# Second four tiles projected in the front of an attention and expert kernel, and a group's sums copied out of their bank in one instruction

## The chip, the cores and the metric

The kernel runs on one core of a Trainium2 chip. Its engines are named as in the profile: PE (TensorE, matmuls; PEld is its loading of weights), DVE (VectorE), ACT (ScalarE), POOL (GpSimd) and SP (SyncE, which here issues transfers). The metric is the device time of one execution in microseconds, as the median of several executions. Beside it there is one profiled execution, whose trace gives every instruction's start and duration.

## The reference

Two residual layers over `x` of 2 x 1024 tokens and 256 features, everything in fp32:

```python
x = x + attn(layernorm(x))      # 16 query heads, 4 key/value heads of 16 features
x = x + ffn(layernorm(x))       # shared expert + 60 experts, top 4

# attn
q = rms_norm(x @ q_kernel); k = rms_norm(x @ k_kernel); v = x @ v_kernel
q, k = rope(q), rope(k)                                   # per head of 16
probs = softmax(einsum('btkgh,bskh->bkgts', q / 4, k))    # no mask
out = einsum('bkgts,bskh->btkgh', probs, v).reshape(B, T, 256) @ out_kernel

# ffn
shared = (silu(x @ g.T) * (x @ u.T)) @ d.T * sigmoid(x @ shared_gate.T)
weights, sel = top_k(softmax(x @ gate.T), 4)
out = shared + sum over the 60 experts of cw_e * ((silu(x @ w1_e.T) * (x @ w3_e.T)) @ w2_e.T)
```

## The kernel before, in words

Tokens are cut into 16 tiles of 128, of which the first eight are batch 0. Tiles are projected in sets of four (`RB`). Set 0 is projected in the front by `project_first`; sets 1 to 3 are projected by the generator `project`, a piece at a time, between the steps of attention.

**The front.** PE multiplies the identity by itself five times (`warm`, line 253), subtracts the weights' means (`center`), and projects set 0: queries to two score buffers (`pq`, `project_to`, line 274), keys and values to a third (`pk`). ACT squares the queries for their norms, copies keys and values out (`kv`, line 409) and squares the keys. DVE takes the variances of x, turns queries and keys (rope), and runs a Newton iteration for the inverse roots (`norm`). PE meanwhile runs 11 more matmuls on the identity, transposes the padded keys (`ktp`, line 345), runs 7 more on the identity, and transposes the scaled queries (`qtp`, line 358). ACT and DVE copy the transposes to `kT` and `qT`, and DVE writes the values, times their norm, to `vaug` (line 335).

**The steps of attention.** There are 128, in the order batch, half of the queries (`qb`), `jp`, `jj`, and key tile `s` (eight). A step has four score matmuls, each on its own 32 rows of the array and 512 queries wide (line 545), into two of three score buffers of two banks each; two exponentials on ACT, 128x1024 each (line 560); and four averages with `vaug`, each on its own 32 columns of the array, summed over the eight steps of a group in the one bank of `ps_av` (line 1068). PE's order is: scores of step r+1, then one piece of other work (`fill`; not in a group's last step, nor in step 1), then the averages of step r. The pieces come from a list: set 1 from step 0 on, then sets 2 and 3, later the output projection and the routing of tokens.

For set 1 the pieces were: keys and values projected to the `misc` bank (`pk`), copied by DVE (line 451), turned and squared, variances (step 0); key transposes (steps 2 and 3), the norm and `vaug` with the first of them; queries of two tiles projected (`pq`), copied by DVE to `u` (line 492) and squared, with half of their turning on POOL (steps 4 and 5); the queries' norm; scaling and query transposes. The `misc` bank is one for all.

**The end of a group.** After a group's eighth step the sums hold numerators and denominators of four heads in turn. With `jj` 0, DVE copies them to `num` (line 578) and later shuffles `num` to `den`. With `jj` 1, DVE copies the odd rows over `num` under a mask (line 585) and shuffles the sums into `den2` (line 586), both out of the bank; the rest (a masked copy, four reciprocals, two products to `encT`) stands in the list `slow`, from which one piece is taken after each of the next seven steps. The output projection reads `encT` nine and ten steps after a group's end with `jp` 1 and `jj` 1. After the last step the list is emptied at once, and PE goes on with the shared expert, where two more output projections are put between.

PE, ACT, DVE and POOL keep the order in which the code names their instructions. SP issues the inputs in front, tiles 4 to 7 of the transposed x (line 144) after the small tables, and then the clearing of the experts' buffers. Behind attention come half of the shared expert, the ranks of the experts, the 60 experts, and the other half of the shared expert.

Of the kernel before, what the change touches and what calls it, by code (L numbers as in the profile page):

```python
# [16 lines left out]
P = 128  # L17
# [6 lines left out]
QB = 512  # L24
# [27 lines left out]
def attention_moe_kernel(  # L52
# [196 lines left out]
    def warm(n):  # L249

        to = bank(P, "warm")
        for _ in range(n):
            nc.tensor.matmul(to, lhsT=ident, rhs=ident, start=True, stop=True)
# [55 lines left out]
        return rope_sb[:, tiles[0] % TPB : tiles[0] % TPB + len(tiles), :]  # L309

    def key_tiles(n):
        kv = pj.tile([P, RB, 2, NKV, H], F32, tag="kv", bufs=1, name=f"kv{n}")
        k1 = pj.tile([P, RB, NKV, H], F32, tag="k1", bufs=1, name=f"k1_{n}")
        k2 = pj.tile([P, RB, NKV, H], F32, tag="k2", bufs=1, name=f"k2_{n}")
        return kv, k1, k2

    def turn_keys(tiles, uk, k1, k2):

        pos = rope_of(tiles)
        nc.vector.tensor_tensor(  # L320
            k1, uk, pos[:, :, None, 0:H].to_broadcast([P, RB, NKV, H]), ALU.mult
        )
        for to, fr, s0 in TURNS:
            nc.vector.tensor_tensor(
                k2[:, :, :, to : to + HH],
                uk[:, :, :, fr : fr + HH],
                pos[:, :, None, s0 : s0 + HH].to_broadcast([P, RB, NKV, HH]),
                ALU.mult,
            )
        pad = kpad[tiles[0] // RB % 2][:, :, H:].rearrange("p t (g w) -> p t g w", g=NKV)  # L330
        nc.vector.tensor_add(pad[:, :, :, 0:H], k1, k2)
# [9 lines left out]
    def keys(tiles, jj, bank, copy):  # L341

        tp = bank(RB * P, f"ktp{tiles[0]}_{jj}").rearrange("p (t n) -> p t n", t=RB)
        for k in range(RB):
            nc.tensor.transpose(
                tp[:, k, :], kpad[tiles[0] // RB % 2][:, k, H - H * jj :][:, 0:P], ident
            )
        c0 = tiles[0] % TPB * P
        copy(
            kT[tiles[0] // TPB][:, jj, c0 : c0 + RB * P], tp.rearrange("p t n -> p (t n)")  # L350
        )
# [15 lines left out]
    def project_first():  # L367


        tiles = range(RB)  # L370
        pos = rope_of(tiles)
        two = [P, 2, NH, H]
        pq = {}
        for k in range(0, RB, 2):
            pq[k] = any_bank(2 * NH * H, f"pq{k}").rearrange("p (t n) -> p t n", t=2)
            for t in range(2):
                project_to(pq[k][:, t], k + t, 0, NH * H)
        variance(tiles)
        t2 = pj.tile([P, RB, NH * H], F32, tag="t2", bufs=1, name="t2_0")
        for k in range(0, RB, 2):  # L380
            for t in range(2):
                sq = pj.tile([P, NH * H], F32, tag="sq", bufs=1, name=f"sq{k + t}")
                nc.scalar.activation(
                    sq,
                    pq[k][:, t],
                    AF.Square,
                    scale=(NH * H) ** -0.5,
                    accum_out=ss[:, 0, k + t : k + t + 1],
                )
            of_k = pos[:, k : k + 2]  # L390
            q1 = pj.tile([P, 2, NH * H], F32, tag="q1", name=f"q1_{k}")
            nc.vector.tensor_tensor(
                heads(q1), heads(pq[k]), of_k[:, :, None, 0:H].to_broadcast(two), ALU.mult
            )
            for to, fr, s0 in TURNS:
                nc.vector.tensor_tensor(
                    heads(t2[:, k : k + 2])[:, :, :, to : to + HH],
                    heads(pq[k])[:, :, :, fr : fr + HH],
                    of_k[:, :, None, s0 : s0 + HH].to_broadcast([P, 2, NH, HH]),
                    ALU.mult,  # L400
                )
            (nc.vector if k else nc.gpsimd).tensor_tensor(
                t2[:, k : k + 2], q1, t2[:, k : k + 2], ALU.add
            )
        pk = any_bank(RB * 2 * NKV * H, "pk0").rearrange("p (t n) -> p t n", t=RB)
        for k in tiles:
            project_to(pk[:, k], k, NH * H, 2 * NKV * H)
        kv, k1, k2 = key_tiles(0)
        nc.scalar.copy(kv.rearrange("p t w g h -> p t (w g h)"), pk)
        for k in tiles:  # L410

            sq = pj.tile([P, NKV * H], F32, tag="sqk1", bufs=1, name=f"sqk{k}")
            nc.scalar.activation(
                sq,
                kv[:, k, 0].rearrange("p g h -> p (g h)"),
                AF.Square,
                scale=NKV**-0.5,
                accum_out=ss[:, 1, k : k + 1],
            )
        warm(11)  # L420
        turn_keys(tiles, kv[:, :, 0], k1, k2)
        keys(tiles, 0, any_bank, nc.scalar.copy)
        keys(tiles, 1, any_bank, nc.scalar.copy)
        warm(7)
        norm(tiles, 0, 3)
        for k in tiles:
            r = rqk[:, 0, k : k + 1]
            if k < 2:
                nc.vector.tensor_scalar_mul(t2[:, k], t2[:, k], r)
            else:  # L430
                nc.scalar.activation(t2[:, k], t2[:, k], AF.Copy, scale=r)
        for k in tiles:
            queries(k, 1, t2[:, k : k + 1], any_bank, (nc.vector.tensor_copy, nc.scalar.copy)[k % 2])
        values(tiles, kv)

    def project(tiles):

        copy = nc.vector.tensor_copy
        set_ = tiles[0] // RB
# [2 lines left out]
        if b == 1:  # L442
            for k in range(0, RB, 2):
                variance(tiles[k : k + 2])
                yield

        pk = bank(RB * 2 * NKV * H, f"pk{set_}").rearrange("p (t n) -> p t n", t=RB)
        for k, i in enumerate(tiles):
            project_to(pk[:, k], i, NH * H, 2 * NKV * H)
        kv, k1, k2 = key_tiles(set_)  # L450
        copy(kv.rearrange("p t w g h -> p t (w g h)"), pk)
        uk = kv[:, :, 0]
        of_k = uk.rearrange("p t g h -> p t (g h)")

# [26 lines left out]
                values(tiles, kv)  # L481
            yield

        u = pj.tile([P, RB, NH * H], F32, tag="u", bufs=1, name=f"u{set_}")

        t2 = pj.tile([P, RB, NH * H], F32, tag="t2", bufs=1, name=f"t2_{set_}")
        pos = rope_of(tiles)
        for k in range(0, RB, 2):
            pq = bank(2 * NH * H, f"pq{tiles[k]}").rearrange("p (t n) -> p t n", t=2)
            for t in range(2):  # L490
                project_to(pq[:, t], tiles[k + t], 0, NH * H)
            copy(u[:, k : k + 2], pq)  # L492
            for t in (k, k + 1):
                sq = pj.tile([P, NH * H], F32, tag="sq", bufs=1, name=f"sq{tiles[t]}")
                nc.vector.scalar_tensor_tensor(
                    sq,
                    u[:, t],
                    1.0 / (NH * H),
                    u[:, t],
                    ALU.mult,  # L500
                    ALU.mult,
                    accum_out=ss[:, 0, tiles[t] : tiles[t] + 1],
                )
            for to, fr, s0 in TURNS:
                for t in (k, k + 1):
                    nc.gpsimd.tensor_tensor(  # L506
                        heads(t2[:, t : t + 1])[:, 0, :, to : to + HH],
                        heads(u[:, t : t + 1])[:, 0, :, fr : fr + HH],
                        pos[:, t, None, s0 : s0 + HH].to_broadcast([P, NH, HH]),
                        ALU.mult,  # L510
                    )
            yield
# [59 lines left out]
    def group_end(av, encT, jp, jj):  # L572

        nonlocal num, den
        if jj == 0:
            num = ends_of.tile([P, QB], F32, tag="num", bufs=2, name="num")
            den = ends_of.tile([P, QB], F32, tag="den", bufs=2, name="den")
            nc.vector.tensor_copy(num, av)
            slow.append(lambda d=den, n=num: nc.vector.stream_shuffle(d, n, SWAP))
            return  # L580
        while slow:
            slow.pop(0)()
        n, d = num, den
        den2 = ends_of.tile([P, QB], F32, tag="den2", bufs=1, name="den2")
        nc.vector.copy_predicated(n, odd_sb.to_broadcast([P, QB]), av)
        nc.vector.stream_shuffle(den2, av, SWAP)  # L586
        slow.append(lambda: nc.vector.copy_predicated(d, odd_sb.to_broadcast([P, QB]), den2))
        for c in range(0, QB, P):
            slow.append(lambda c=c: nc.vector.reciprocal(d[:, c : c + P], d[:, c : c + P]))
            if c // P % 2:  # L590
                h = slice(c - P, c + P)
                slow.append(lambda h=h: nc.vector.tensor_mul(encT[:, jp, h], n[:, h], d[:, h]))
# [403 lines left out]
    with tc.manual_schedule(engines={mybir.EngineType.PE}), ExitStack() as both:  # L996
# [6 lines left out]
        warm(5)  # L1003
        center(0, NH * H)
        center(NH * H, 3 * P)
        project_first()
        late = project(range(RB, TPB))

# [382 lines left out]
```

## Time and profile before

| | us |
|---|---|
| median of three runs | 678.12 (677.0 to 678.4) |
| the profiled execution itself | 678.74 |
| its span on the core | 676.9 |
| front, up to the first score matmul | 19.8 |
| PE busy in 0 to 19.8, of 19.8 | 16.60 |
| PE busy in 19.8 to 46 (26.2 long) | 25.83 |
| PE busy in 155 to 290 (135 long), ACT in the same | 133.54, 112.05 |
| PE busy in 400 to 640 (240 long) | 236.84 |
| the end of the chain that ended last | shared expert on PE, from 614.5 to 673.3 |

In the lines of the timeline the columns are start, length, engine, line, operation, output and inputs, shape, and the number of instructions merged; in brackets is the engine's idle time before it and who ended it. A long score or projection matmul in fp32 has two records. The waits give who waited for whom, the total, how often and the longest. Rows of one line give count, shortest/median/longest duration in ns, and the first and last start in us.

### The profile page before, as it was taken

The page shows a single profiled execution, that of the slowest core. Times are in us where ns is not written, and L with a number is a line of the kernel's source. Part 1 is how long each engine was busy: PE and PEld are TensorE (multiplying, and loading weights), DVE is VectorE, ACT ScalarE, POOL GpSimd, SP SyncE. Part 2 cuts the span into 40 slices and gives each one's busy share as a digit, 9 for nine tenths or more (in the row PEclk, how much of TensorE's full clock was granted, in tenths as well). Part 3 has the DMA queues.
Part 4 walks back from the last instruction along what each step waited for, and adds up shares of the span by engine and source line. Part 5 has one row for each costly group of instructions (what it writes and reads, how often), then busy time and mean ns, then how long its engine had stood idle before and what let it go on. Part 6 is the DMA issues. An engine that isn't in the chain of part 4 may idle for free. (4 is left out here: it accounts for less than half of the span.)

```text
span 676.9 us, 12425 instructions
## 1 busy us (share of the span) xinstructions
PE 663.9 (98%) x4156; PEld 375.9 (56%) x4157; DVE 361.7 (53%) x1404; ACT 355.7 (53%) x503; POOL 185.7 (27%) x250
## 2 busy tenths in 40 slices
PE   8999999999999999999999998999999999999997
PEld 7432332442224223233235477898998989885466
DVE  5653755427154376556657755444444434543984
ACT  3678778768986787877862400333333333332210
POOL 4020020011000034533135451444444454543000
PEclk9999999999999999999999999999999999999999
DMA  8999930002100011211011084799989899933951
GB/s 274 294 285 298 333 124 1 1 1 92 42 1 1 0 43 42 75 51 50 9 51 66 34 317 163 252 292 296 298 284 307 286 287 293 299 90 113 309 178 48
DMA packets 64275, 106.33 MB, mean 157 GB/s; under 512 B 7417, under 2 KB 51209, under 8 KB 64210
## 3 DMA queue, kind: packets, MB, share of 16 engines
q1 hardware_dynamic: 55010, 86.57, 39.6%
q0 software_dynamic: 7680, 17.32, 7.4%
q10 hardware_dynamic: 1520, 1.64, 0.7%
q8 instruction: 33, 0.54, 0.3%
q14 instruction: 32, 0.26, 0.1%
HBM read 64.13 MB, written 42.45 MB: 157 GB/s over the span
## 5 line engine op out<-in xcount | busy, mean ns | idle before, releaser
L545 PE MATMUL sc<-qT,kT 32*128 32x512 f32 x1024 | 160.3, 639 | 0.8 <-DVE vaug L335 0.5
L560 ACT ACTIVATE ex<-sc,rqk 128x1024 f32<-128x1024 f32 x128 | 134.2, 1111 | 36.8 <-PE sc L545 35.1
L1068 PE MATMUL av<-ex,vaug 128*32 128x512 f32 x1024 | 137.3, 604 | 2.6 <-DVE den L586 1.8
L560 ACT ACTIVATE ex<-sc 128x1024 f32<-128x1024 f32 x128 | 124.1, 1022 | 28.2 <-PE sc L545 24.6
L933 POOL DMA_INDIRECT yt<-ys,dst x96 | 92.8, 966 | 115.2 <-ACT ys L1207 67.5
L545 PEld LDWEIGHTS sc<-qT,kT 32*128 32x128 f32 x1024 | 52.7, 183 | 109.1 <-issue 67.5
L1200 PE MATMUL ye<-w,hbuf 128*128 128x256 f32 (+5 forms) x384 | 93.3, 381 | 0.0
L739 POOL DMA_INDIRECT xg<-xs,idx x64 | 63.3, 989 | 100.7 <-DVE idx L734 73.5
L863 PE MATMUL sg<-x2T,ws_sb 128*128 128x512 f32 x176 | 78.1, 596 | 1.2 <-ACTq L1278 1.2
L917 PE MATMUL gua<-xT,w 128*128 128x128 f32 (+5 forms) x480 | 73.2, 295 | 0.5 <-DVE xT L1188 0.5
L917 PEld LDWEIGHTS gua<-xT,w 128*128 128x128 f32 x480 | 70.1, 191 | 4.8 <-issue 0.6
L1207 ACT COPY ys<-ye 128x256 f32<-128x256 f32 (+5 forms) x60 | 29.9, 499 | 73.0 <-PE ye L1200 47.4
L1200 PEld LDWEIGHTS ye<-w,hbuf 128*128 128x128 f32 (+5 forms) x384 | 58.9, 164 | 14.5
L1068 PEld LDWEIGHTS av<-ex,vaug 128*32 128x32 f32 x1024 | 20.4, 107 | 79.0 <-issue 66.1
L925 DVE TENSOR_TENSOR hbuf<-hbuf,gua 128x128 f32<-128x128 f32 (+5 forms) x60 | 18.9, 315 | 85.0 <-ACT hbuf L924 45.9
L863 PEld LDWEIGHTS sg<-x2T,ws_sb 128*128 128x128 f32 x176 | 32.6, 190 | 38.9 <-issue 35.5
L924 ACT ACTIVATE hbuf<-gua 128x128 f32<-128x128 f32 (+5 forms) x60 | 17.9, 299 | 64.7 <-PE gua L917 41.8
L506 POOL TENSOR_TENSOR t<-u,rope_sb 128x128 f32<-128x128 f32 x24 | 12.4, 545 | 129.5 <-DVE u L492 129.5
L873 ACT ACTIVATE hs<-sg 128x512 f32<-128x512 f32 (+1 forms) x24 | 14.3, 596 | 59.0 <-PE sg L863 56.7
L885 PE MATMUL so<-ws_sb,hs 128*128 128x256 f32 x192 | 42.5, 381 | 1.5 <-DVE acc L893 1.5
L917 PE MATMUL gub<-xT,w 128*112 128x128 f32 (+5 forms) x240 | 41.2, 294 | 0.0
L885 PEld LDWEIGHTS so<-ws_sb,hs 128*128 128x128 f32 x192 | 36.2, 190 | 8.2 <-DVE acc L893 2.2
(184 smaller groups left out, 663.1 us busy)
## 6 DMA issues: line engine op xcount, KB each, us to landing
w<-in_wexp_dram SPq DMA_DIRECT2D x60, 624.0 KB
xg<-void SPq DMA_DIRECT2D x60, 221.0 KB
yt<-zero SPq DMA_DIRECT2D x32, 256.0 KB
got<-yt SPq DMA_DIRECT2D x16, 512.0 KB
xe<-xg SPq DMA_DIRECT2D x24, 136.0 KB
xe<-xg SPq DMA_DIRECT2D x10, 170.0 KB
yt<-ys,dst POOLq DMA_INDIRECT x96
xe<-xg SPq DMA_DIRECT2D x8, 187.0 KB
```

Source lines behind the costliest of these rows:

```text
L545: nc.tensor.matmul(sc[:, gg, :], lhsT=kT[b][r : r + 32, jj, s0 : s0 + P], rhs=qT[b][r : r + 32, jp, t0 : t0 + QB], start=True, stop=True,)
L560: nc.scalar.activation(ex, sc, AF.Exp, scale=rqk[:, 1, i : i + 1] if b == 0 else 1.0)
L739: s = nc.gpsimd.indirect_dma_start(out=xg[:, :], out_offset=bass.IndirectOffsetOnAxis(ap=at_, axis=0), in_=xs[:, i, :], in_offset=None, bo ...
L863: nc.tensor.matmul(p, lhsT=ws1_sb[:, c, c0 : c0 + P], rhs=x2T[:, c, n * FB : (n + 1) * FB], start=c == 0, stop=c == CC - 1,)
L885: nc.tensor.matmul(po, lhsT=hs[:, m, t * P : (t + 1) * P], rhs=ws2_sb[:, m, :], start=m == 0, stop=m == NC2 - 1,)
L917: nc.tensor.matmul(ps[part][0:m, 0:n], lhsT=w[:, c * W1C + c0 : c * W1C + c0 + m], rhs=xT[:, c, 0:n], start=c == 0, stop=c == CC - 1,)
L924: nc.scalar.activation(h[:, 0, 0:n], ps["ga"][:, 0:n], AF.Silu)
L925: nc.vector.tensor_mul(h[:, 0, 0:n], h[:, 0, 0:n], ps["ua"][:, 0:n])
L933: s = nc.gpsimd.indirect_dma_start(out=yt[:, :], out_offset=bass.IndirectOffsetOnAxis(ap=at, axis=0), in_=y, in_offset=None, bounds_check= ...
L1068: nc.tensor.matmul(av[32 * g : 32 * g + 32, :], lhsT=vaug[:, b * TPB + s, g, H * jj : H * jj + 32], rhs=es[g // 2][:, g % 2, :], start=s == 0,
L1200: nc.tensor.matmul(po[:, t, :], lhsT=h[:, k, t * rows : (t + 1) * rows], rhs=w[:, CC * W1C + k * C : CC * W1C + (k + 1) * C], start=k == 0 ...
L1207: nc.scalar.copy(ys, po)
```

## The change

`project_first` now also projects set 1. After the squares of set 0's keys, PE projects set 1's keys and values to the `misc` bank, which ACT copies to a second `kv` tile, and the queries of tiles 4 and 5 to a score buffer, which ACT copies to `u`. Then come set 0's key transposes, then the queries of tiles 6 and 7 to the `misc` bank, which ACT copies to `u` behind its last copy of query transposes. The 11 and the 7 matmuls on the identity are gone. `project` gets `kv` and `u` of set 1 handed in, and leaves out the projections and DVE's three copies for it; its pieces stay in the same steps, and those of steps 4 and 5 have no matmuls left. `kv` has two buffers (the pool's number) in the place of one.

At a group's end with `jj` 1 DVE copies the sums to a tile `both`; the masked copy and the shuffle read that tile, and are one more piece at the head of `slow`, which has eight pieces then.

```diff
@@ -309,10 +309,9 @@
         return rope_sb[:, tiles[0] % TPB : tiles[0] % TPB + len(tiles), :]
 
     def key_tiles(n):
-        kv = pj.tile([P, RB, 2, NKV, H], F32, tag="kv", bufs=1, name=f"kv{n}")
         k1 = pj.tile([P, RB, NKV, H], F32, tag="k1", bufs=1, name=f"k1_{n}")
         k2 = pj.tile([P, RB, NKV, H], F32, tag="k2", bufs=1, name=f"k2_{n}")
-        return kv, k1, k2
+        return k1, k2
 
     def turn_keys(tiles, uk, k1, k2):
 
@@ -405,7 +404,8 @@
         pk = any_bank(RB * 2 * NKV * H, "pk0").rearrange("p (t n) -> p t n", t=RB)
         for k in tiles:
             project_to(pk[:, k], k, NH * H, 2 * NKV * H)
-        kv, k1, k2 = key_tiles(0)
+        kv = pj.tile([P, RB, 2, NKV, H], F32, tag="kv", name="kv0")
+        k1, k2 = key_tiles(0)
         nc.scalar.copy(kv.rearrange("p t w g h -> p t (w g h)"), pk)
         for k in tiles:
 
@@ -417,11 +417,24 @@
                 scale=NKV**-0.5,
                 accum_out=ss[:, 1, k : k + 1],
             )
-        warm(11)
-        turn_keys(tiles, kv[:, :, 0], k1, k2)
-        keys(tiles, 0, any_bank, nc.scalar.copy)
-        keys(tiles, 1, any_bank, nc.scalar.copy)
-        warm(7)
+
+        ahead = range(RB, TPB)
+        pk = bank(RB * 2 * NKV * H, "pk1").rearrange("p (t n) -> p t n", t=RB)
+        for k, i in enumerate(ahead):
+            project_to(pk[:, k], i, NH * H, 2 * NKV * H)
+        kv_a = pj.tile([P, RB, 2, NKV, H], F32, tag="kv", name="kv1")
+        nc.scalar.copy(kv_a.rearrange("p t w g h -> p t (w g h)"), pk)
+        u_a = pj.tile([P, RB, NH * H], F32, tag="u", bufs=1, name="u1")
+        pq_a = {}
+        for k, to in ((0, any_bank), (2, bank)):
+            pq_a[k] = to(2 * NH * H, f"pq{RB + k}").rearrange("p (t n) -> p t n", t=2)
+            for t in range(2):
+                project_to(pq_a[k][:, t], ahead[k + t], 0, NH * H)
+            if k == 0:
+                nc.scalar.copy(u_a[:, 0:2], pq_a[0])
+                turn_keys(tiles, kv[:, :, 0], k1, k2)
+                keys(tiles, 0, any_bank, nc.scalar.copy)
+                keys(tiles, 1, any_bank, nc.scalar.copy)
         norm(tiles, 0, 3)
         for k in tiles:
             r = rqk[:, 0, k : k + 1]
@@ -431,9 +444,12 @@
                 nc.scalar.activation(t2[:, k], t2[:, k], AF.Copy, scale=r)
         for k in tiles:
             queries(k, 1, t2[:, k : k + 1], any_bank, (nc.vector.tensor_copy, nc.scalar.copy)[k % 2])
+        nc.scalar.copy(u_a[:, 2:4], pq_a[2])
         values(tiles, kv)
-
-    def project(tiles):
+        return kv_a, u_a
+
+    def project(tiles, kv=None, u=None):
+
 
         copy = nc.vector.tensor_copy
         set_ = tiles[0] // RB
@@ -443,12 +459,14 @@
             for k in range(0, RB, 2):
                 variance(tiles[k : k + 2])
                 yield
-
-        pk = bank(RB * 2 * NKV * H, f"pk{set_}").rearrange("p (t n) -> p t n", t=RB)
-        for k, i in enumerate(tiles):
-            project_to(pk[:, k], i, NH * H, 2 * NKV * H)
-        kv, k1, k2 = key_tiles(set_)
-        copy(kv.rearrange("p t w g h -> p t (w g h)"), pk)
+        if kv is None:
+
+            pk = bank(RB * 2 * NKV * H, f"pk{set_}").rearrange("p (t n) -> p t n", t=RB)
+            for k, i in enumerate(tiles):
+                project_to(pk[:, k], i, NH * H, 2 * NKV * H)
+            kv = pj.tile([P, RB, 2, NKV, H], F32, tag="kv", name=f"kv{set_}")
+            copy(kv.rearrange("p t w g h -> p t (w g h)"), pk)
+        k1, k2 = key_tiles(set_)
         uk = kv[:, :, 0]
         of_k = uk.rearrange("p t g h -> p t (g h)")
 
@@ -481,15 +499,18 @@
                 values(tiles, kv)
             yield
 
-        u = pj.tile([P, RB, NH * H], F32, tag="u", bufs=1, name=f"u{set_}")
+        made = u is not None
+        if not made:
+            u = pj.tile([P, RB, NH * H], F32, tag="u", bufs=1, name=f"u{set_}")
 
         t2 = pj.tile([P, RB, NH * H], F32, tag="t2", bufs=1, name=f"t2_{set_}")
         pos = rope_of(tiles)
         for k in range(0, RB, 2):
-            pq = bank(2 * NH * H, f"pq{tiles[k]}").rearrange("p (t n) -> p t n", t=2)
-            for t in range(2):
-                project_to(pq[:, t], tiles[k + t], 0, NH * H)
-            copy(u[:, k : k + 2], pq)
+            if not made:
+                pq = bank(2 * NH * H, f"pq{tiles[k]}").rearrange("p (t n) -> p t n", t=2)
+                for t in range(2):
+                    project_to(pq[:, t], tiles[k + t], 0, NH * H)
+                copy(u[:, k : k + 2], pq)
             for t in (k, k + 1):
                 sq = pj.tile([P, NH * H], F32, tag="sq", bufs=1, name=f"sq{tiles[t]}")
                 nc.vector.scalar_tensor_tensor(
@@ -581,9 +602,16 @@
         while slow:
             slow.pop(0)()
         n, d = num, den
+
+        both = ends_of.tile([P, QB], F32, tag="both", bufs=1, name="both")
         den2 = ends_of.tile([P, QB], F32, tag="den2", bufs=1, name="den2")
-        nc.vector.copy_predicated(n, odd_sb.to_broadcast([P, QB]), av)
-        nc.vector.stream_shuffle(den2, av, SWAP)
+        nc.vector.tensor_copy(both, av)
+
+        def take():
+            nc.vector.copy_predicated(n, odd_sb.to_broadcast([P, QB]), both)
+            nc.vector.stream_shuffle(den2, both, SWAP)
+
+        slow.append(take)
         slow.append(lambda: nc.vector.copy_predicated(d, odd_sb.to_broadcast([P, QB]), den2))
         for c in range(0, QB, P):
             slow.append(lambda c=c: nc.vector.reciprocal(d[:, c : c + P], d[:, c : c + P]))
@@ -1003,8 +1031,7 @@
         warm(5)
         center(0, NH * H)
         center(NH * H, 3 * P)
-        project_first()
-        late = project(range(RB, TPB))
+        late = project(range(RB, TPB), *project_first())
 
 
 
```

## The prediction

> **What bounds the kernel now.** I began with the busy shares, then TensorE's waits, and then its order of time in the two stretches that the change touches.
>
> ```profile
> PE   663.9 (98%) x4156; PEld 375.9 (56%) x4157; DVE 361.7 (53%) x1404; ACT 355.7 (53%) x503; POOL 185.7 (27%) x250
> PEclk9999999999999999999999999999999999999999
> ```
>
> TensorE (PE) has a record open 98% of the span and VectorE (DVE) and ScalarE (ACT) have half their time free, so only what shortens or lengthens PE's queue counts. The clock is full everywhere. But "busy" includes stalls inside a group of matmuls, so I read PE in order of time. First the front, and the first score steps:
>
> ```profile
> 12.25 2.62 PE L253 MATMUL warm<-ident 128*128 128x128 f32 x22
> 15.24 1.06 PE L345 MATMUL ktp<-ident,kpad 128*128 128x128 f32 x8 [0.37 <-DVE kpad L331]
> 16.14 1.73 PE L253 MATMUL warm<-ident 128*128 128x128 f32 x14
> 17.89 1.46 PE L358 MATMUL qtp<-ident,t 128*128 128x128 f32 x8
> 19.82 1.99 PE L545 MATMUL sc<-qT,kT 32*128 32x512 f32 x12 [0.46 <-DVE vaug L335]
> 22.16 1.13 PE L545 MATMUL sc<-qT,kT 32*128 32x512 f32 x4 [0.36 <-ACT ex L560]
> 23.21 2.05 PE L274 MATMUL pk<-wqkv_sb,xT_sb 128*128 128x128 f32 x16
> 25.20 1.06 PE L1068 MATMUL av<-ex,vaug 128*32 128x512 f32 x8
> ...
> 35.54 1.99 PE L274 MATMUL pq<-wqkv_sb,xT_sb 128*128 128x256 f32 x8
> 37.46 1.07 PE L1068 MATMUL av<-ex,vaug 128*32 128x512 f32 x8
> 38.46 1.14 PE L545 MATMUL sc<-qT,kT 32*128 32x512 f32 x8
> 39.53 1.99 PE L274 MATMUL pq<-wqkv_sb,xT_sb 128*128 128x256 f32 x8
> ```
>
> From 12.25 to 17.89 PE has nothing to do but the key transposes; DVE is making the keys, the norms and the scaled queries, and 18 filler matmuls pass the time. From 23.21 the projections of tiles 4 to 7 stand between scores and their averages. Next, steps with no inserted work:
>
> ```profile
> 174.04 1.46 PE L545 MATMUL sc<-qT,kT 32*128 32x512 f32 x8
> 175.44 1.06 PE L1068 MATMUL av<-ex,vaug 128*32 128x512 f32 x8
> 176.43 1.14 PE L545 MATMUL sc<-qT,kT 32*128 32x512 f32 x8
> 177.50 1.06 PE L1068 MATMUL av<-ex,vaug 128*32 128x512 f32 x8
> 178.50 1.46 PE L545 MATMUL sc<-qT,kT 32*128 32x512 f32 x8
> ```
>
> Every second score group takes 1.39 us start to next start where the others take 1.07. There are three score buffers and two per step, so every second group must wait for an exponential to end. Two steps take 4.46 where PE's work is 4.13: without inserted work PE loses 0.33 per two steps to ACT. What is taken out of a score stretch is thus not all won.
>
> Last, the end of a group of eight steps whose sums go to the odd heads:
>
> ```profile
> PE av L1068 <- DVE den L586: 1.8, 4, 0.5
> L578 DVE COPY num<-av x8: 691/692/693, 47.0 to 332.0; 128x512 f32<-128x512 f32 x8
> L585 DVE COPY_PREDICATED num<-odd_sb,av x8: 728/730/734, 65.7 to 349.6; 128x512 f32<-128x512 int32 x8
> L586 DVE STREAM_SHUFFLE den<-av x8: 719/728/730, 66.3 to 350.2; 128x512 f32<-128x512 f32 x8
> ```
>
> Two DVE instructions read the only sum bank one after the other (about 1.36 us in all), and the next group's first average waits for them behind a score group of 1.07.
>
> [...] 100% busy in the unfilled steps above with 0.33 of 4.46 us lost. [...] the four score matmuls of a step take 1.07 us together, and the first exponential starts only 0.1 us after the records of all four end; a group cut in two by a buffer wait costs 0.33 more. [...] Fillers may go if real work takes their place; in the new front I find no PE gap above 0.5 us, and the clock reads 1.00 in every stretch now. [...] the new copy should cost what the even-group copy does, 0.69. That row has the same shape.
>
> **The change part by part.** I write S for the first score matmul (19.82 now).
>
> *Front.* Filler of 2.62 and 1.73 goes. In come 16 passes of pk (2.05 long in the row; in a row of its kind in front the pitch is 0.112, so 1.79), and two sets of 8 pq passes at a pitch of 0.216, 1.73 each. PE: pk1 12.25 to 14.04, first pq to 15.77. The keys are ready at 15.09, so their transposes (0.90 from start to the next) now wait for PE: 15.77 to 16.67. Second pq to 18.40. The scaled queries are ready at 17.8, so the query transposes start 0.50 late. From there it is a chain as now (transpose, DVE copy, fourth transpose in the same bank, ACT copy, S: 1.92 us), so S = 20.32. ACT gets three copies of 128x512 (0.59 in row L409): kv at about 14.6, after the key squares; the first u at 15.97 to 16.55, ahead of the two key copies (to about 17.6) and the two query scalings (to about 18.5). The fourth transpose needs that at about 19.4, so it is covered; without 0.9 us of cover it would push S. The second u copy stands after the query copies and before the first exponential, in the 1.2 us that ACT now waits for the first scores. DVE's order up to there is unchanged. The inputs of tiles 4 to 7 arrive at 10.5 and are wanted at 12.25. Cost: +0.5, between +0.2 and +1.3.
>
> *Score stage, r = 0 to 6.* Out go pk (1.98 between neighbours) and twice pq (1.92). First pk: after the second score group PE goes to the first average at 23.21, where its exponentials have ended at 23.11: the whole 1.98 is won. DVE's keys and variances of tiles 4 to 7 no longer wait for pk (it idled 5.1 us for that) and are done long before their transposes. From key transposes to copy, norm, exponential of step 4 (29.65 to 33.31) the chain is the same and moves with PE. Then the two pq: without them scores of step 6 follow at once, their exponentials trail, and step 7's scores fall into the stalled position that the pq hid. Step by step with 1.07, 1.00 and 0.33: step 6 is 1.92 earlier, step 7 3.85, step 8 3.54, step 12 3.54. So 2 x 1.92 - 0.33 = 3.5, and 5.5 with pk. Bounds: 6.0 if no stall appears, 4.5 if three more do.
>
> DVE also loses three copies (3 x 0.69) that nothing waits for.
>
> *Group ends.* The bank is free after one copy of 0.69, inside the 1.07 of the score group, so these waits go. Measured from the end of the score group to the average, they are 0.57, 0.57, 0.26, 0.34, 0.57 and 0.57 in ends one to six; at the seventh the inserted transposes cover it, and after the eighth no average comes. But where the score group before was an unstalled one (the 0.57s), the next then stalls: 0.33 back in the first batch, 0.23 in the second, whose exponentials are shorter (1.02 against 1.11). Net 0.24, 0.24, 0.26, 0.34, 0.34, 0.34 = 1.75. Bounds: 0.8 (half taken by ACT) to 2.9 (no stall). The selecting copy and the shuffle move to the next step's slot, from SBUF; the trace has that kind in L587, 0.73. They are eight times 0.69 more for DVE, hidden by its idle half. The chain now has eight pieces and seven slots, so the last product slips to the step that starts the output projection; the matmuls that read it come a step later, about 1 us after it. At the end of attention the last sums are 0.61 later on DVE: their first product ends at 354.55 instead of 353.94 and PE asks for it at 354.70. Covered by 0.15; beyond that it is lost one for one.
>
> Behind the attention stage nothing is tied to absolute time: the clearing transfers end near 90 us, scatters, ranks and weights follow PE's steps. So the sum passes on: +0.5 - 5.5 - 1.75 = -6.75. The profiled execution took 678.74 (span 676.9 and 1.8 around it), so 672.0 for one like it; the median of the runs is 0.6 lower, 678.12, so 671.4.
>
> **The rivals.** (1) ACT sets the pace: the pairs of steps at 4.46 show that it does without inserted work. If the group ends give 0.8 and the removed projections only 4.5: -4.8, 673.3. For it: the 0.27 that ACT idles per two steps is all its slack. Against: the stretch still holds transposes and a wait for norms. (2) The front is longer because ACT's copies come in the order kv, u, keys, queries: S +1.3, sum -5.95, 672.2. (3) More won: no new stalls, -8.0, 670.1; against it, every unfilled pair of steps shows them. (4) Slower: the projections in front wait for the input transfer of tiles 4 to 7. It shares the queue with other loads and is issued at 5.84. It must land after 10.5 + 1.7 (slack) + 6.75 + 1.4 = 20.4 us to make the kernel slower by over 0.2%. Against: in the trace it landed at 10.5, with only small loads before it and nothing in the change moved in that queue.
>
> **How the numbers follow.** Step sum as worked out 68%, (1) 14%, (2) 6%, (3) 4%, nothing measurable 3%, (4) or another loss 5%. Under 0.2% (1.4 us) this kernel's runs, spread over 1.4 us, tell nothing. Faster 0.92, same 0.03, slower 0.05. The likeliest is 671.4; 669.8 to 673.8 takes in its bounds, rivals (1) to (3) and the spread of runs.
>
> **What would show it.** Right: first scores near 20.3; first average about 3.4 after them without pk; step 12's scores near 49.0 instead of 54.01; no wait of an average for the sum's shuffle; the last output projection without a wait; spans of shared and expert stages unchanged. Wrong: a wait of pk for a transfer before 14, a query transpose later than 18.8, more than one long score group in two, or waits for the copied sums.

## The result, and the profile after

| us | before | after |
|---|---|---|
| median of the runs side by side | 678.26 (677.0 to 678.5) | 670.58 (669.12 to 671.15) |
| the profiled execution | 678.74 | 669.12 |
| its span | 676.87 | 666.99 |

The ratio is 0.9885, 95% interval 0.9869 to 0.9902: 7.7 us less. Predicted were 671.4 and a range of 669.8 to 673.8.

First the page of the profile after, busy shares and TensorE's clock:

```profile
PE   658.5 (99%) x4120; PEld 372.7 (56%) x4121; DVE 365.9 (55%) x1409; ACT 357.5 (54%) x506; POOL 185.7 (28%) x250
PEclk9999999999999999999999999999999999999999
```

PE has 36 matmuls less (the 18 fillers, two records each) and stays busy to 99%; DVE has 4.2 us more, ACT 1.8. The clock is full, as before, once it has risen: the nines hide the start, where PE's first five matmuls on the identity take 2.50 us, 0.50 each, while eleven take 2.62 from 12.25 us on in before. Then PE's timeline of after, in the front and the first steps (start, length, engine, line, operation, shape, matmuls merged, idle time before):

```profile
9.98 3.73 PE L274 MATMUL pk<-wqkv_sb,xT_sb 128*128 128x128 f32 x32
13.55 1.89 PE L274 MATMUL pq<-wqkv_sb,xT_sb 128*128 128x256 f32 x8
15.28 1.04 PE L344 MATMUL ktp<-ident,kpad 128*128 128x128 f32 x8
16.15 1.89 PE L274 MATMUL pq<-wqkv_sb,xT_sb 128*128 128x256 f32 x8
17.88 1.42 PE L357 MATMUL qtp<-ident,t 128*128 128x128 f32 x8
19.76 1.99 PE L566 MATMUL sc<-qT,kT 32*128 32x512 f32 x12 [0.46 <-ACT qT L359]
22.10 1.13 PE L566 MATMUL sc<-qT,kT 32*128 32x512 f32 x4 [0.36 <-ACT ex L581]
23.16 1.07 PE L1095 MATMUL av<-ex,vaug 128*32 128x512 f32 x8
...
33.49 1.06 PE L1095 MATMUL av<-ex,vaug 128*32 128x512 f32 x8
34.49 1.14 PE L566 MATMUL sc<-qT,kT 32*128 32x512 f32 x8
35.56 1.06 PE L1095 MATMUL av<-ex,vaug 128*32 128x512 f32 x8
36.56 1.46 PE L566 MATMUL sc<-qT,kT 32*128 32x512 f32 x8
...
48.44 1.14 PE L566 MATMUL sc<-qT,kT 32*128 32x512 f32 x8
```

Real work stands where the fillers stood, with no idle time until the query transposes are through. The first average follows the first scores by 3.40 us (before 5.38, with `pk` between). Where step 4's and 5's `pq` stood, scores and averages now alternate, with every second score group long again. Step 12's scores come 28.68 us after the first (before 34.19); the prediction had 49.0 - 20.3 = 28.7.

At a group's end the bank is free after one copy. The instructions on the tile `both` (count, shortest/median/longest in ns, first and last start):

```profile
L608 DVE COPY both<-av x8: 691/692/692, 60.1 to 342.2; 128x512 f32<-128x512 f32 x8
L611 DVE COPY_PREDICATED num<-odd_sb,both x8: 718/728/750, 62.0 to 342.9; 128x512 f32<-128x512 int32 x8
L612 DVE STREAM_SHUFFLE den<-both x8: 730/740/766, 62.7 to 343.6; 128x512 f32<-128x512 f32 x8
```

The copy costs the 0.69 of its even twin; reading the tile rather than the bank changed neither of the other two by more than 0.012 us (0.73 and 0.74). In PE's list of waits the 1.8 us for the shuffle is gone; what is left of averages waiting is 0.2 us.

By stages the two profiled executions, and a second one of each kernel (its own run, below), compare so. "Front" is from the first matmul of set 0's keys to the first score matmul, "scores" from there to the first matmul of the shared expert:

| us | before | before, 2nd | after | after, 2nd |
|---|---|---|---|---|
| up to the first keys | 10.47 | 10.40 | 9.98 | 10.80 |
| front | 9.35 | 9.69 | 9.78 | 9.77 |
| scores | 329.63 | 329.63 | 322.33 | 322.30 |
| shared expert, ranks, up to the first expert | 68.41 | 67.92 | 66.22 | 67.87 |
| experts | 195.16 | 195.97 | 195.09 | 195.87 |
| last half of the shared expert | 63.86 | 63.86 | 63.60 | 63.60 |
| span | 676.87 | 677.47 | 666.99 | 670.20 |

Only three rows hold the change. The score stage repeats within 0.03 us and is 7.30 shorter, the front is 0.1 to 0.4 longer, the last stage 0.26 shorter. The front's second value of before is the odd one: there the key transposes wait 0.7 us for DVE where they wait 0.4 in the first. The two further profiles below that leave the front's order as in before and keep the clock full there have 9.34 and 9.35, and every profile with the whole new front has 9.76 to 9.78. The start varies by 0.8 and the shared stage by 2, with one and the same kernel. So the profiled execution of after is 2 us luckier than its change.

The start follows the moment at which PE's clock first rises to full. By the clock records of the traces that is 4.91 us in after, 5.76 and 5.90 in the two profiles of before, and 7.51 in the second of after; the first keys come at 9.98, 10.40, 10.47 and 10.80. The matmuls for the weights' means (`wmean`), which start at 4.3 us, take 1.77 us where the clock rises at 4.91, 2.26 where it rises at 5.90, and 2.77 where it rises at 7.51. The change has no part in this.

### The profile page after: what moved, and what is told of

The parts are those of the page before. It is cut to its first block, busy times and chain, and to the rows that moved or that the text cites. A ratio compares the mean times of both kernels' runs of the same rounds, so it can differ in the third digit from the quotient of the medians.

```text
span 667.0 us, 12351 instructions
## 1 busy us (share of the span) xinstructions
PE 658.5 (99%) x4120; PEld 372.7 (56%) x4121; DVE 365.9 (55%) x1409; ACT 357.5 (54%) x506; POOL 185.7 (28%) x250
## 3 DMA queue, kind: packets, MB, share of 16 engines
q10 hardware_dynamic: 1520, 1.64, 0.7%
## 5 line engine op out<-in xcount | busy, mean ns | idle before, releaser
L1095 PEld LDWEIGHTS av<-ex,vaug 128*32 128x32 f32 x1024 | 20.3, 108 | 77.8 <-issue 65.5
```

Of the source, the lines that this page charges most:

```text
L1095: nc.tensor.matmul(av[32 * g : 32 * g + 32, :], lhsT=vaug[:, b * TPB + s, g, H * jj : H * jj + 32], rhs=es[g // 2][:, g % 2, :], start=s == 0,
```

## The experiments

All kernels are run beside the kernel before; "scores" is the stage of the table.

**The two parts alone.** After, with the old group ends:

```diff
-        nc.vector.tensor_copy(both, av)
-
-        def take():
-            nc.vector.copy_predicated(n, odd_sb.to_broadcast([P, QB]), both)
-            nc.vector.stream_shuffle(den2, both, SWAP)
-
-        slow.append(take)
+        nc.vector.copy_predicated(n, odd_sb.to_broadcast([P, QB]), av)
+        nc.vector.stream_shuffle(den2, av, SWAP)
```

> The front and the score steps as changed, the group ends as before. The sum of the prediction gives +0.5 in the front and -5.5 in steps 0 to 12: -5.0, about 673.3. Waits of averages for the shuffle of the sums stay (about 2 us of idle time in the trace). Rival (the exponentials take most of what leaves the score steps): no more than -3, 675 or above.

And before, with the new group ends (the same lines the other way round):

> The group ends as changed, the front as before. The sum gives -1.75: 676.5; no average waits for the sums in the trace, and one more score group in each batch is stalled behind ends that were unstalled. Rival (the waits go but the exponentials take it all): within 0.5 of the kernel before, 678. Rival (DVE's extra copies are on the path): slower, 679 or above.

| | median, us | ratio to before, 95% | front | scores |
|---|---|---|---|---|
| new front alone | 674.2 | 0.9926 [0.9908, 0.9943] | 9.76 | 324.10 |
| new ends alone | 677.14 | 0.9961 [0.9945, 0.9976] | 9.35 | 327.86 |

In the score stage the front change gives 329.63 - 324.10 = 5.53 and the ends 329.63 - 327.86 = 1.77. Together 7.30, which is what both give: the parts do not touch each other.

The 0.26 of the last stage belongs to neither part alone. PE's wait at the start of that stage falls from 1.16 us to 0.89 with either part (the stage takes 63.61 with the new front alone), and with the ends alone 0.2 comes back further on (63.78). Why was not found.

**The two kernels again.** Both as they are, for the scatter of a stage:

> The changed kernel once more. From the first score matmul to the shared expert's first matmul its trace was 7.3 us shorter than before, and the stretch from there to the first expert 2.2 us shorter, which no part of the change accounts for. Theory A (that stretch differs between executions of any kernel): this profile can read 66.2 or 68.4 us there, and the time is 670 to 672. Theory B (the change shortens it): 66.2 again, here and in the kernel with the group ends alone, and 68.4 in both kernels with the old group ends.

> The kernel before once more, for the spread of two equal kernels: ratio 1.000 within 0.002. Theory A: the stretch from the shared expert's first matmul to the first expert reads anything between 66 and 69 us; theory B: 68.4 as in the first profile.

After: 672.36, ratio 0.9888 [0.9869, 0.9907]; before: 679.16, ratio 0.9994 [0.9982, 1.0007]. The shared stage of after took 67.87 this time. Over the fourteen profiles of this study it took 66.22 in four and 67.8 to 68.5 in ten; kernels with the old front and kernels with the new one are in both groups. The long ones have this line in PE's list of waits (total, times, longest), here of the second execution of after; the first has none:

```profile
PE so L913 <- DVE acc L921: 1.4, 1, 1.4
```

Once in the stage DVE's addition of an output tile comes late and holds its bank. What delays it was not found.

**The bank held longer.** After, with the sums copied out twice:

```diff
         nc.vector.tensor_copy(both, av)
+        both2 = ends_of.tile([P, QB], F32, tag="both2", bufs=1, name="both2")
+        nc.vector.tensor_copy(both2, av)
```

> The changed kernel with the sums copied twice out of their bank at each end of the odd heads, so that the bank is held for 1.30 us in the place of 0.69. If the hold is what the group ends paid for: the waits come back, 0.06 shorter than before, and the stretch from the first score to the shared expert is 322.3 + 1.4 = 323.7. Rival (the gain came from the two instructions leaving DVE's queue ahead of other work): 322.3.

Measured: 673.18, ratio 0.9915 [0.9899, 0.9931], scores 323.69, 1.36 more than after. And the wait is back, in PE's list:

```profile
PE av L1097 <- DVE both L610: 1.5, 4, 0.4
```

Two reads of 0.69 exceed the score group of 1.07 that covers one, and the list names the second read (L610), so it is the hold and not DVE's added work elsewhere. Before, six score groups at the ends take 1.64 to 1.65 us to the next start; here the same six take 1.57, and in after none of them does. The gain of the ends is thus the time the bank is held. DVE's one added copy costs PE nothing that shows: in the score stage of after no wait for DVE is in PE's list.

**What ScalarE's pace is worth.** After, with one constant scale in all exponentials. In batch 0 this leaves out the norm of the keys; batch 1 had a constant before, and only its value changes:

```diff
-nc.scalar.activation(ex, sc, AF.Exp, scale=rqk[:, 1, i : i + 1] if b == 0 else 1.0)
+nc.scalar.activation(ex, sc, AF.Exp, scale=0.05)
```

> The changed kernel with a constant in the place of the keys' norm in the exponentials of batch 0, which leaves that norm out; the exponential with a constant takes 1.02 us in batch 1 where the one with the norm takes 1.11. If the stall of every second score group is the wait for one exponential, it falls from 0.33 to 0.24 in 26 groups of batch 0, and the wait for the norm in step 4 goes too: 322.3 - 2.3 - 0.3 = 319.7 from the first score to the shared expert. Rival (PE alone sets the pace): 322.3.

Measured: 668.66, ratio 0.985 [0.9831, 0.987]; scores 319.39, so 2.94 less. In the list of groups of after (busy, mean ns, idle before, releaser) one sees both forms of the exponential:

```profile
L581 ACT ACTIVATE ex<-sc,rqk 128x1024 f32<-128x1024 f32 x128 | 134.1, 1111 | 30.1 <-PE sc L566 28.4
L581 ACT ACTIVATE ex<-sc 128x1024 f32<-128x1024 f32 x128 | 124.1, 1021 | 27.2 <-PE sc L566 23.7
```

The 128 instructions with a scale by row take 0.09 us longer each than the 128 with a constant (1.111 against 1.021). What PE loses in its long score groups of batch 0 (start to next start, less 1.07, summed) falls from 8.59 to 5.74; in batch 1 it does not change. This is the 0.33 of two steps that the prediction charged to ACT: ACT idles 30 us in batch 0 and yet sets this part of the pace.

**The fillers.** Before, without them:

```diff
-        warm(11)
-        warm(7)
```

> The kernel before without the 11 and the 7 matmuls on the identity, and nothing in their place. If they only pass the time, PE waits for DVE instead: no change within 0.2% (first scores 9.35 to 9.7 us after the first key projection, as in two profiles of the kernel before). Rival (they hold the clock up): PE is left idle for about 2.9 and 1.7 us, its clock falls, the transposes and the first scores have twice their pitch, and 1.5 to 3 us are lost.

Measured: **683.66**, ratio 1.0059 [1.0045, 1.0073]. The main expectation was wrong, and its rival right in kind and too small. PE's timeline:

```profile
10.78 1.95 PE L274 MATMUL pk<-wqkv_sb,xT_sb 128*128 128x128 f32 x16
15.55 1.06 PE L345 MATMUL ktp<-ident,kpad 128*128 128x128 f32 x8 [2.82 <-DVE kpad L331]
18.20 1.97 PE L358 MATMUL qtp<-ident,t 128*128 128x128 f32 x8 [1.59 <-DVE t L427]
20.64 5.37 PE L543 MATMUL sc<-qT,kT 32*128 32x512 f32 x16 [0.46 <-DVE vaug L335]
25.93 3.78 PE L274 MATMUL pk<-wqkv_sb,xT_sb 128*128 128x128 f32 x16
```

and stretches of it (PE, PEld, DVE, ACT, POOL busy; then the granted clock, the share of the DMA engines, GB/s):

```profile
17.00:18.00 1.00, 0.00 (x0) 0.00 (x0) 0.79 (x5) 0.57 (x2) 0.00 (x0) 0.86 1.03 359
20.00:30.00 10.00, 9.54 (x37) 5.38 (x40) 1.24 (x6) 4.61 (x5) 0.00 (x0) 0.50 0.89 279
31.00:32.00 1.00, 1.00 (x8) 0.31 (x8) 0.96 (x4) 0.00 (x0) 0.00 (x0) 0.81 0.88 281
```

A mean of 0.86 over the microsecond from 17 says that the clock fell to half at about 17.7, and 0.81 over the one from 31 that it rose at 31.4. In these 13.6 us the second `pk` takes 3.78 where it took 2.05. Front and scores are 0.50 and 4.46 longer than before. The gaps themselves cost nothing: PE waits for DVE there in any case (with half the fillers, below, they are 1.71 and 0.92 us, and the front takes 9.34).

**Keys alone in front.** After, with the queries of tiles 4 to 7 left in steps 4 and 5. The front then has `pk` in the place of the first fillers and nothing in the place of the second:

```diff
         nc.scalar.copy(kv_a.rearrange("p t w g h -> p t (w g h)"), pk)
-        u_a = pj.tile([P, RB, NH * H], F32, tag="u", bufs=1, name="u1")
...
-                project_to(pq_a[k][:, t], ahead[k + t], 0, NH * H)
-            if k == 0:
-                nc.scalar.copy(u_a[:, 0:2], pq_a[0])
...
-        nc.scalar.copy(u_a[:, 2:4], pq_a[2])
...
-        return kv_a, u_a
+        return kv_a, None
```

> The changed kernel with the queries of tiles 4 to 7 left in steps 4 and 5, so that only their keys and values go to the front. Front: not longer than before, as 1.79 us fit into the wait for the keys. From the first score to the shared expert: 329.63 - 1.98 (one projection) - 1.77 (group ends, as measured) = 325.9. So 3.5 of the changed kernel's 7.3 us there are the queries, at 0.5 us of front. Rival (the exponentials pay most of it back): above 327.

Measured: 678.44, ratio 0.9979 [0.9959, 0.9998]: nearly all of the gain was gone. The profiled execution again has half the clock, from 17.8 to 31.4, after these gaps, of which none exceeds 1.6 us:

```profile
10.80 3.73 PE L274 MATMUL pk<-wqkv_sb,xT_sb 128*128 128x128 f32 x32
15.58 1.06 PE L344 MATMUL ktp<-ident,kpad 128*128 128x128 f32 x8 [1.04 <-DVE kpad L330]
18.22 1.97 PE L357 MATMUL qtp<-ident,t 128*128 128x128 f32 x8 [1.58 <-DVE t L434]
```

and the stretch from 20 to 30 us:

```profile
20.00:30.00 10.00, 9.54 (x37) 2.58 (x40) 5.09 (x20) 4.61 (x5) 0.00 (x0) 0.50 0.91 283
```

Its twelve runs spread from 674.1 to 680.9, and each run's mean clock sorts them. The three with 0.999 or 1.000 took 674.1 to 675.5, about what had been expected; the two with 0.995, 677.5 and 677.9; the seven with 0.989 to 0.992, 678.4 to 680.9.

**Keys in front, gaps filled.** The same kernel with fillers in the two gaps:

```diff
+        warm(4)
         pk = bank(RB * 2 * NKV * H, "pk1").rearrange("p (t n) -> p t n", t=RB)
...
         keys(tiles, 1, any_bank, nc.scalar.copy)
+        warm(7)
```

> Keys and values of the second four tiles in front, their queries in steps 4 and 5 as before, one copy at a group's end, and fillers in the two gaps that the run with keys alone left open (4 matmuls on the identity ahead of the new projection, 7 ahead of the query transposes). If that run lost its gain to a clock at half speed from 17.9 to 31 us, and to nothing else, the clock reads 1.00 here, from first scores to the shared expert it takes what had been expected there, 327.9 - 2.0 = 325.9 us (it took 330.3), and the run takes about 679.1 - 3.8 = 675.3. If moving the keys alone cost something of its own, the stretch stays above 328.

Measured: 674.16, ratio 0.9952 [0.994, 0.9964], all six runs at 0.999 or 1.000, front 9.34, scores 326.14. Against the kernel before it gains 3.3 us of the median where keys alone gained 0.7; in the profiled executions, of which the one with keys alone had the clock at half, front and scores differ by 0.51 + 4.15. Eleven matmuls that compute nothing do that. The last 3 us before the query transposes are then full, at full clock:

```profile
15.00:18.00 3.00, 3.00 (x28) 2.82 (x26) 2.55 (x16) 2.05 (x5) 0.00 (x0) 1.00 1.01 341
```

In the score stage the clock was all but 0.2 of the loss: 326.14 for the 325.9 worked out without it.

**Half the fillers.** Before, with 5 and 3:

```diff
-        warm(11)
+        warm(5)
-        warm(7)
+        warm(3)
```

> The kernel before with 5 and 3 fillers in the place of 11 and 7. Open gaps of about 1.6 and 1.0 us; TensorE works 2.8 of the 5.5 us from 12.7 to 18.2. With keys alone in front the clock fell although no gap was above 1.6 us, with 0.9 us of work in the 3.7 before the query transposes. If one gap's length decides, the clock falls here too: from first scores to the shared expert 334, 683 in all. If the share of work in some microseconds decides (half here, a quarter there), the clock stays at 1.00 and nothing changes: 329.6 and about 679.

Measured: 677.93, ratio 1.0014 [1.0002, 1.0026]. The profiled execution keeps the full clock and 329.60 in the score stage, with a gap of 1.71 us, longer than any of the kernel with keys alone. But of the fourteen runs three had a mean clock of 0.995 and took 680.3 to 681.0, three had 0.997, and eight 1.000. So neither expectation holds whole: a gap of 1.71 kept the clock in this profile where 1.58 lost it in the other, and with half the work the mean clock was 1.000 in only eight runs of fourteen. Between 12 and 18 us this is how the two kernels stand, first half the fillers, then keys alone:

```profile
12.00:15.00 3.00, 1.83 (x17) 1.63 (x15) 2.82 (x8) 1.99 (x10) 1.22 (x1) 1.00 0.92 307
15.00:18.00 3.00, 1.74 (x14) 1.58 (x14) 2.55 (x15) 1.37 (x3) 0.00 (x0) 1.00 1.01 355
```

```profile
12.00:15.00 3.00, 2.54 (x23) 2.35 (x21) 2.86 (x8) 2.14 (x11) 1.27 (x1) 1.00 0.92 314
15.00:18.00 3.00, 1.06 (x8) 0.85 (x8) 2.54 (x15) 1.70 (x4) 0.00 (x0) 0.96 0.94 327
```

In the last 3 us before the query transposes PE works 1.74 in the one and 1.06 in the other.

**A faster version?** After the run with a constant scale, I took the norm out of half of batch 0's exponentials in earnest. The keys are scaled in their padded tile before the odd heads' transposes: the first four tiles' in step 0, the second four's in step 2 behind norm and values. The first four's transposes move from the front to step 4, the second four's stay in step 3:

```diff
+    def scale_keys(tiles):
+        pad = kpad[tiles[0] // RB % 2][:, :, H:].rearrange("p t (g w) -> p t g w", g=NKV)
+        r = rqk[:, 1, tiles[0] : tiles[0] + RB]
+        nc.vector.tensor_tensor(
+            pad[:, :, :, 0:H],
+            pad[:, :, :, 0:H],
+            r[:, :, None, None].to_broadcast([P, RB, NKV, H]),
+            ALU.mult,
+        )
...
-                keys(tiles, 1, any_bank, nc.scalar.copy)
...
             variance(tiles)
+            scale_keys(range(RB))
...
                 values(tiles, kv)
+                scale_keys(tiles)
...
         for k in range(0, RB, 2):
+            if b == 0 and k == 0:
+                keys(range(RB), 1, bank, copy)
...
-                nc.scalar.activation(ex, sc, AF.Exp, scale=rqk[:, 1, i : i + 1] if b == 0 else 1.0)
+                nc.scalar.activation(ex, sc, AF.Exp, scale=rqk[:, 1, i : i + 1] if b == 0 and jj == 0 else 1.0)
```

> After, with the keys of batch 0 scaled by their norm (in the padded tile, one DVE instruction for each four tiles) before the transposes for the odd heads, which move to steps 3 and 4; the exponentials of the odd groups take a constant scale then. Exponentials with a constant scale in all of batch 0 brought 2.9 us in the run with the constant; half of them should bring 1.4, so 320.9 from first scores to the shared expert (322.3 after), the front 0.0 to 0.3 shorter, and about 669 in all. If the two added transposes' steps or DVE's added work lie on the path, it is 322 or more.

Measured: 671.37, ratio 0.9908 [0.9894, 0.9922], scores 325.48. Its timeline on PE shows a wait, and the stretches a clock at half, from 32.9 to 36.3:

```profile
29.41 1.14 PE L579 MATMUL sc<-qT,kT 32*128 32x512 f32 x8
32.76 0.99 PE L354 MATMUL ktp<-ident,kpad 128*128 128x128 f32 x4 [2.21 <-DVE kpad L335]
33.68 1.94 PE L1108 MATMUL av<-ex,vaug 128*32 128x512 f32 x8
```

```profile
33.00:34.00 1.00, 1.00 (x8) 0.55 (x10) 0.21 (x1) 0.61 (x1) 0.00 (x0) 0.50 0.92 286
```

The second four's transposes waited for the norm, the values and the scaling on DVE. With the two sets of transposes otherwise placed (the first four's in step 3, the second four's in step 5):

```diff
-            keys(tiles, jj, bank, copy)
+            keys(range(RB) if b == 0 and jj == 1 else tiles, jj, bank, copy)
...
+            if b == 0 and k == 2:
+                keys(tiles, 1, bank, copy)
```

> The same as the run with scaled keys, but with the odd heads' key transposes a step or more later: those of the first four tiles in step 3 (their keys are scaled in step 0), those of the second four in step 5. There the second four's stood in step 3, waited 2.21 us for DVE's norm and scaling, and the clock was half from 32.9 to 36.3. If that was all that ate the gain, no transpose waits for DVE here, the clock reads 1.00 in the steps, and from first scores to the shared expert it takes 322.3 - 1.4 = 320.9 us, about 669 in all (ratio 0.986). If constant scales in half the groups bring nothing, it is 322.3 or more.

Measured: 671.28, ratio 0.9883 [0.9867, 0.99]. No transpose waits, the clock reads 0.999 to 1.000 in all runs, and the score stage takes 321.97: 0.36 less than after, not 1.4. The long score groups of batch 0 lose 7.41 us, 1.18 less, so the shorter exponentials did bring most of what was expected. But the first four's transposes, moved out of the front, now take 0.59 of PE in the score stage; the expectation had forgotten them. Front and scores together come to 331.32, against 332.11 and 332.07 in the two executions of after. In the time of whole runs it can't be told from after.

## Why the prediction was right

**Front.** +0.5 was forecast, +0.43 measured against the first profile of before and +0.09 against the second, in which DVE was late. The order on PE and ACT is the one worked out. The query transposes start 7.90 us after the first keys where they started 7.42: 0.48 late, for the 0.50 of the prediction. ACT's second copy of `u` stands in the gap before the first exponential. No projection waits for the transfer of tiles 4 to 7, so the rival on the slower side had no place; it was not tried with a late transfer.

**Score steps.** -5.5 was forecast, -5.53 measured. The run with keys in front and gaps filled splits it: against the ends alone, keys bring 327.86 - 326.14 = 1.72 (forecast 1.98), and the queries a further 326.14 - 322.33 = 3.81 (forecast 3.52). The new long score group was forecast at 0.33: batch 0 loses 8.59 after and 8.27 in that run, 0.32 more. The run with keys in front also loses 0.27 more than after in batch 1's long groups (6.46 against 6.19), where neither part does anything. Without that the split would be 1.99 and 3.54, close to the forecast.

**Group ends.** -1.75 was forecast, -1.77 measured, and holding the bank for another 0.69 gave 1.36 of it back. The values were forecast end by end, and by batch they sum to 0.74 and 1.02. With the ends alone, the time lost in score groups is 0.74 less in batch 0 than before and 1.02 less in batch 1; so the forecast that ACT takes 0.33 or 0.23 back at some ends held too. Within a batch the ends were not read one by one. The output projections behind attention, at 347.34 and 352.50, run without a wait.

**What follows behind.** "Spans of shared and expert stages unchanged" holds within their scatter. The last stage's -0.26 was not foreseen. From the traces the change is +0.43 - 7.30 - 0.26 = -7.1; the medians gave 7.7 and 6.9 in the two comparisons, the sum predicted 6.75.

**The rivals.** Rival (1), ACT sets the pace, is out at its size: the score stage lost none of the 5.5 and 1.75 to ACT beyond what the sum had set aside. The long groups of batch 0 lose 8.6 us after and 9.0 before, but by the prediction's own reading 1.4 of the 9.0 (0.57, 0.57 and 0.26) were waits for the sum bank. ACT's part thus grew from 7.6 to 8.6, for 3 x 0.33 forecast. Rivals (2) and (3) would show as a front longer by 1.3 or as score steps without the new long group; neither is in the trace. The sum given for (3) is also off: with the prediction's bounds of 6.0 and 2.9 it is -8.4, not -8.0.

**What the prediction undervalued.** It said that 18 filler matmuls "pass the time", and further on, "Fillers may go if real work takes their place". The second was right, and it was the point on which everything hung: with neither the fillers nor the work the kernel takes 683.7. The prediction's step was safe because it puts work into both gaps, not because it is useful work. Its sum has no term for the clock. Had the change moved only the keys, the same sum would have forecast about 675, and missed by 3 us, with gaps of only 1.04 and 1.58 us.

## What to carry to other kernels

Before you take out work that computes nothing, ask what PE does in the few microseconds around it, and put real work in its place gap by gap; moving only the keys in front gained 0.7 us with the gaps left open and 3.3 with them filled. Split a sum by stages whose durations repeat to 0.03 us: the parts added up exactly there, while whole runs scattered by 2 us. Where a result bank is read by two instructions and the cover is one score group, copy it once and let the rest read the copy; DVE's added 0.69 was free here, where DVE is idle for nearly half the span, but every matmul moved to a stage that PE fills is paid in full, four transposes included.

## What the runs showed of the hardware

**The clock fell with gaps of 1.0 to 2.8 us.** It read 0.50 with gaps of 1.04 and 1.58 us (keys alone, from 17.8 to 31.4), with 2.82 and 1.59 (without fillers, from 17.7 to 31.4), and with a single gap of 2.21 (the first version with scaled keys, from 32.9 to 36.3). It stayed at 1.00 with 1.71 and 0.92 in the profile with half the fillers.

**Equal kernels differ in it.** The clock first rose anywhere from 4.91 to 7.51 us after the kernel's start. The kernel with keys alone had a mean clock of 1.000 in one run and of 0.989 in another.

**What decides was not shown.** PE's busy time in two stretches of 3 us before the query transposes, in four profiles:

| run | PE busy, 12 to 15 us | PE busy, 15 to 18 us | clock |
|---|---|---|---|
| without fillers | 0.73 | 1.06 | falls at 17.7 |
| keys alone | 2.54 | 1.06 | falls at 17.8 |
| half the fillers | 1.83 | 1.74 | stays at 1.00 |
| keys in front, gaps filled | 2.94 | 3.00 | stays at 1.00 |

In the second stretch the two that lost the clock had the least work, but in the first 0.73 us of work went by at full clock. And with half the fillers six of fourteen runs lost some clock (0.995 or 0.997), though the profiled one lost none. That PE's work counts and not the longest gap is the author's estimate, from these profiles alone.

**How long it stays at half is open.** It was 3.4 us with scaled keys and 13.6 with keys alone and without fillers, though PE was busy all 9.00 us from 21 to 30 in both of these. Why was not found.

**The price.** 13.6 us at half clock cost 5.0 us without fillers (0.50 in the front and 4.46 in the score stage). If PE's pace alone decided, it would be half of 13.6, 6.8 us, as an estimate. The difference is presumably time in which PE waits for DVE and ACT anyway; it was not taken apart.
